# Attention b: where the rows that hold a softmax's maxima are cleared, written and copied

## The chip, the cores and the metric

The kernel runs on one core of a Trainium2 chip. The metric is the time of one execution on the device in microseconds. The core has five engines that work side by side: PE multiplies matrices and transposes, DVE, ACT and POOL do vector work, and SP only issues transfers (DMAs). Each engine runs its instructions in order; an instruction that waits holds up all that is queued behind it on that engine.

## The reference

Four layers on x of 2 x 512 x 512 (batch, sequence, width), each added to its input behind a layer norm:

```python
x = L0_attn_a_hidden_states
x = x + _L0_attn_a_ref(_layernorm(x), ...)   # 32 heads of 128, 8 for keys and values, int4 weights
x = x + _L0_ffn_ref(_layernorm(x), ...)      # 8 experts of rank 64, the best 2 of each row
x = x + _L0_attn_b_ref(_layernorm(x), Wq, Wk, Wv, Wo)
x = x + _L0_ffn_ref(_layernorm(x), ...)      # the same experts
```

The change lies in attention b, which has heads of only 16 elements:

```python
q = (resid @ Wq).reshape(B, T, 32, 16)       # k and v: 8 heads, each shared by 4 of q
q, k = q * cos + rotate_half(q) * sin, k * cos + rotate_half(k) * sin
att = einsum('bhgqd,bhkd->bhgqk', q, k) / sqrt(16)
probs = softmax(where(causal, att, -inf))
out = einsum('bhgqk,bhkd->bhgqd', probs, v).reshape(B, T, 512) @ Wo
```

## The kernel before

**Stages.** Attention a runs from 0 to about 735 us, with the first experts of batch 0 mixed in near its end, and is not touched. Then come the first experts of batch 1 (`experts(1, "f1")`) with the projections of attention b for batch 0 (to about 809 us), the loop of attention b (to about 1056 us), and a tail: the output projection of the last heads (`output_b(1, (2, 3))`) and the second experts of batch 1. The experts of batch 0 for the second time, the projections of batch 1 and the rest of the output projection are *side work*: generators from which the loop takes some units in each step.

**What the loop does.** It goes over 32 pairs of heads `p` = (batch b, half of the key heads `kh`, group `g`, `pr`), three steps a pair. A pair's softmax needs each row's maximum before the exponentials, and both the maximum and the subtraction are brought into matmuls. A query is kept as a high part, rounded to PE's fast 32-bit form (`fp32r`), and the low rest; keys likewise. Four copies of 16 rows (query high, low, high, low against key high, high, low, low) make 64 rows, so that one matmul over them has all four products. Behind these lie two more rows (`HALF` = 64 to `HM` = 66): -1 in the keys' tile `ks` (L588), and in the queries' tile `qs` first zeros, later the row's maximum as a high and a low part. So a matmul with zeros there gives the scores, and one with the maxima there gives scores less the maximum. For each pair, in the order of its life:

- `queries_halved(p)` (L724 to 733), once per four pairs, at a step in which another pair's load is due: ACT rounds the queries to `hl` (L729), POOL takes the low rest (L730), and two transfers (`spread`, L711) write both to a buffer in DRAM, each row twice. The pool `dram` has two buffers for each such name.
- `queries_in(p)` (L735 to 740), four steps ahead of the pair's first step: one transfer loads 64 rows of 4 KB into `qs[p % 5]`; from the sixth pair on POOL clears rows 64 and 65 (L740), since an earlier pair has left its maxima there.
- `maxima()` (L742 to 774), three steps: PE's `sc_b` (L758) are scores of the queries against the keys up to the diagonal, for query tiles 0 and 1 in the first step, 3 in the second and 2 in the third. DVE reduces each to its rows' maxima, `top` (L762). Behind the last, POOL writes the maxima's high part (L770) and low part (L771) to two columns of `mm`, first of one head, then of the other: columns 64 and 65 for the first head, 0 and 1 for the second.
- `maxima_in(p)` (L776 to 784), at step 3p + 4 (`step - 4` in the loop), ahead of that step's other work on PE: four transpositions of `mm` into one bank, `tpm` (L781), and one ACT copy for each head from there to `qs` (L784).
- `probabilities()` (L789 to 825), from step 3p + 8 (`LEAD`): `st_b` (L805), keys against queries with the maxima's rows; ACT's exponential to `pT_b` (L811); POOL's causal mask on the diagonal tiles (L814).
- `weighted_b` (L824 to 855): `num_b` (L831), values and a column of ones against `pT_b`, for two pairs at a time; its results' denominators go by `dens_b` transfers to one tile. Then `divided` (L860 on: two reciprocals on DVE, and what they multiply) and `output_b` (L878 on).

**What sets the order.** Inside the loop PE's order is the one written in the program (`manual_schedule`, PE alone); the other engines' order is placed by a scheduler from the dependencies. In a step PE gets: `maxima_in`, then the step's `st_b`, its `sc_b`, the `num_b` that are due, and then side work. How much of that is set by `pace`, added to `left` in every step; each unit of side work takes its own worth away, mostly `MM` = 0.9. The pace is 1.05 at the start, 0.38 from step 44, 1.05 from step 66 and 1.5 from step 90; the loop has 96 + 8 steps. After the last step some side work (`parts(side, 6)`) stands ahead of `output_b(1, (2, 3))`, which needs the last quotients.

**Rings.** `qs` has five tiles, `mm` two. `sc_b`, `st_b` and `tpm` share five banks of PSUM (`ps_x`); side work in the loop has two others (`ps_f`), and outside the loop it uses the five. `we` (L254) holds the gate's weight of each expert, spread over its 64 ranks, for one tile of 128 rows; POOL writes it, PE transposes it to `wT_f`. Its pool has two tiles for the four of a batch. `pT_b` tiles 512 wide have a ring of five.

The lines around the step that moves:

```python
            p, at = divmod(step - 4, STEPS)
            if at == 0 and 0 <= p < len(pairs):
                maxima_in(p)
            if LEAD <= step:
                next(ps)        # probabilities: st_b
            if step < total:
                next(ms)        # maxima: sc_b
```

Of the kernel before, what the change touches and what calls it, by code (L numbers as in the profile page):

```python
# [11 lines left out]
F32 = mybir.dt.float32  # L12
# [7 lines left out]
P = 128  # L20
# [20 lines left out]
def kernel(  # L41
# [533 lines left out]
    HALF, HM = P // 2, P // 2 + 2  # L575
# [11 lines left out]
    for pad in ks:  # L587
        nc.gpsimd.memset(pad[HALF:HM], -1.0)  # L588
# [10 lines left out]
    dram = ctx.enter_context(tc.tile_pool(name="dram", bufs=2, space=bass.MemoryType.DRAM))  # L599
    ptp = ctx.enter_context(tc.tile_pool(name="pT2", bufs=6))  # L600
# [3 lines left out]
    homes.update(xT=(xtp, "xnT"), xn=(temps, "t"), hT=(hp, "hT"), we=(wep, "we"))  # L604
# [102 lines left out]
    def spread(hl, nm, order):  # L707

        to = dram.tile([4, P, S], F32, tag=f"spread{nm[0]}", name=f"spread_{nm}")
        for twice in range(2):  # L710
            nc.sync.dma_start(  # L711
                to[order[twice]].rearrange("n r s -> r n s"), hl.bitcast(F32)
            )
        return to.rearrange("n (d h) s -> (n d) h s", h=B_NKV)

    kparts, qparts = {}, {}

    def keys_in(b, kh):

        if kh == 0:  # L720
            kparts[b] = spread(khls[b], f"k_{b}", (slice(0, 4, 2), slice(1, 4, 2)))
        nc.sync.dma_start(ks[kh][:HALF], kparts[b][:, ts(kh, 4), :])

    def queries_halved(p):  # L724

        b, kh, g, _ = pairs[p]
        hl = hlp.tile([P, 2, S], F32R, tag="hl", name=f"hl_{p}")
        src = qTs[b][:, kh * 2 + g // 2, :]
        nc.scalar.copy(hl[:, 0, :], src)  # L729
        nc.gpsimd.tensor_tensor(hl[:, 1, :], src, hl[:, 0, :].bitcast(F32), ALU.subtract)  # L730
        to = spread(hl, f"q_{p}", (slice(0, 2), slice(2, 4)))
        for n in range(4):
            qparts[p + n] = to

    def queries_in(p):  # L735
        _, _, g, pr = pairs[p]
        q = qs[p % NQ]
        nc.sync.dma_start(q[:HALF], qparts.pop(p)[:, ts((g % 2) * 2 + pr, 2), :])
        if p >= NQ:
            nc.gpsimd.memset(q[HALF:HM], 0.0)  # L740

    def maxima():  # L742

        for p, (b, kh, g, pr) in enumerate(pairs):
            q, k = qs[p % NQ].bitcast(F32R), ks[kh].bitcast(F32R)
            top = small.tile([P, NT, 2], F32, tag="top", name=f"top_{p}")
            for tiles in ((0, 1), (3,), (2,)):
# [18 lines left out]
                if tiles == (2,):  # L766
                    mm = mms[p] = mmp[p % len(mmp)]
                    for h in range(2):
                        at = (1 - h) * HALF
                        nc.gpsimd.tensor_copy(mm[:, :, at], top[:, :, h])  # L770
                        nc.gpsimd.tensor_tensor(  # L771
                            mm[:, :, at + 1], top[:, :, h], mm[:, :, at].bitcast(F32), ALU.subtract
                        )
                yield

    def maxima_in(p):  # L776

        mm = mms.pop(p).bitcast(F32)
        tp = ps_x.tile([P, S], F32, tag="x", name=f"tpm_{p}")
        for t in range(NT):  # L780
            nc.tensor.transpose(tp[:HM, ts(t, P)], mm[:, t, :], ident)  # L781
        for h in range(2):
            at = (1 - h) * HALF
            nc.scalar.copy(qs[p % NQ][HALF:HM, h, :].bitcast(F32R), tp[at : at + 2, :])  # L784
# [136 lines left out]
    banks[:] = BESIDE  # L921
    side = chain(later, projections(1))
    pace, left = 1.05, 0.0
    for step in range(total + LEAD):
        with tc.manual_schedule(engines={mybir.EngineType.PE}):
# [8 lines left out]
            if step == half + LEAD + 10:  # L934
                side = chain(side, output_b(0, (2, 3)), experts(0, "f2", True))
                pace, left = 1.05, 0.0
            if step == total - 6:
                side = chain(output_b(1, (0, 1)), side)
                pace, left = 1.5, 0.0
# [6 lines left out]
            p, at = divmod(step - 4, STEPS)  # L946
# [22 lines left out]
    parts(side, 6)  # L969
    run(output_b(1, (2, 3)))  # L970
    run(side, experts(1, "f2", True))
# [90 lines left out]
```

## Time and profile before

| | |
|---|---|
| median of three runs | 1117.19 us (1116.21 to 1117.54) |
| the profiled execution, its time | 1118.06 us |
| its span, first to last instruction | 1116.3 us |
| mean granted clock of PE | 0.992 of full speed |
| PE busy | 1060.7 us, 95% of the span, 4940 instructions |
| PE's weight loads (beside its matmuls) | 708.8 us, 63% |
| DVE busy | 880.8 us, 79% |
| ACT busy | 617.4 us, 55% |
| POOL busy | 587.4 us, 53% |
| chain that ended last, by engine | PE 80%, DVE 10%, ACT 3%, POOL 3%, issue 2%, DMA 1% |

By stage, busy us of each engine:

| stretch, us | what | length | PE | DVE | ACT | POOL | clock |
|---|---|---|---|---|---|---|---|
| 0 to 735 | attention a | 735 | 704.7 | 646.9 | 439.1 | 430.3 | 1.00 |
| 736 to 808 | first experts of batch 1, projections of batch 0 | 72 | 68.3 | 36.6 | 15.3 | 27.9 | 0.98 |
| 808 to 832 | start of the loop | 24 | 21.1 | 20.6 | 11.7 | 8.4 | 0.79 |
| 832 to 1056 | the rest of the loop | 224 | 212.5 | 150.1 | 142.9 | 118.5 | 1.00 |
| 1056 to 1117 | tail | 61 | 53.1 | 25.6 | 8.4 | 2.3 | 0.96 |

An engine's busy time is the time in which it executes something; the rest of a stretch it waits, for another engine, a bank, a transfer or its own order. The clock is the share of its full speed that PE was granted. In the groups, `qs<-tpm 2x512` is an operation that reads `tpm` and writes `qs`, 2 partitions by 512 elements; a name after `<-` in a wait is the engine and the tile that ended it.

### The profile page before, as it was taken

The numbers are of one execution on the slowest core, as the hardware profiler recorded it, in microseconds if no ns is written. First come the engines' busy times: TensorE is split into PE (matmuls) and PEld (weight loads), VectorE is DVE, ScalarE is ACT, GpSimd is POOL, SyncE is SP. The second block draws the span as 40 slices with busy tenths as digits, with TensorE's granted clock in tenths as the row PEclk, the third lists the DMA queues.
The fourth block names the chain that finished last, engine by engine and source line by source line (L and its number), as shares of the span: only waits on it lengthen the run. The fifth ranks groups of instructions, "written<-read, shape, count | busy, mean of one in ns | idle before, by whom it ended". The sixth has DMA issues, their size and how long they took to land.

```text
span 1116.3 us, 16200 instructions
## 1 busy us (share of the span) xinstructions
PE 1060.7 (95%) x4940; PEld 708.8 (63%) x4940; DVE 880.8 (79%) x2195; ACT 617.4 (55%) x1421; POOL 587.4 (53%) x920
## 2 busy tenths in 40 slices
PE   5799999999999999999999999999989989999988
PEld 3467677777777777777777777546457555555543
DVE  6889899999999999999999889574376677877252
ACT  3556566577566566566565665513157566585410
POOL 2557566666656656756756666261245566454200
PEclk9999999999999999999999999999989999999999
DMA  7301011022010010010021000042342235111000
GB/s 288 114 1 38 1 38 38 1 76 68 9 39 24 15 38 14 26 38 8 32 76 38 1 1 1 1 156 63 91 156 77 61 106 152 44 44 26 10 33 38
DMA packets 21030, 58.11 MB, mean 52 GB/s; under 512 B 3152, under 2 KB 4112, under 8 KB 18128
## 3 DMA queue, kind: packets, MB, share of 16 engines
q1 hardware_dynamic: 20944, 57.08, 15.6%
q8 instruction: 40, 0.66, 0.2%
q14 instruction: 46, 0.38, 0.1%
HBM read 43.30 MB, written 12.58 MB: 50 GB/s over the span
## 4 chain that ended last, share of the span: by engine, by line
PE 80%; DVE 10%; ACT 3%; POOL 3%; issue 2%; DMA 1%; SPq 0%; ACTq 0%; DVEq 0%; POOLq 0%
PE av L429 11%; PE sc L396 11%; PE tp L424 5%; PE ps_o L439 5%; PE ps_o L438 5%; PE ps_q L358 5%; PE ph_f L207 5%; PE ps_q L359 5%; PE num_b L831 3%; PE st_b L805 3%; PE py_f L266 3%; PE sc_b L758 3%; PE pq_b L678 2%; PE po L885 2%; DVE r_q L365 2%
## 5 line engine op out<-in xcount | busy, mean ns | idle before, releaser
L404 ACT ACTIVATE p<-sc,nmx 128x128 f32<-128x128 f32 (+3 forms) x256 | 135.7, 530 | 95.1 <-DVE nmx L399 92.1
L376 POOL TENSOR_TENSOR r_q<-r_q,tab 128x512 f32<-128x512 f32 x64 | 82.5, 1289 | 190.2 <-DVE rs_q L375 190.2
L396 PE MATMUL sc<-kT,qT 128*128 128x128 f32 (+3 forms) x512 | 180.0, 433 | 1.2 <-POOL qT L377 0.9
L365 DVE SCALAR_TENSOR_TENSOR r_q<-ps_q,s_q,r_q 128x512 f32<-128x512 f32 x192 | 143.4, 747 | 36.1 <-PE ps_q L359 22.4
L413 POOL TENSOR_SCALAR p<-p,rden 128x128 f32<-128x128 f32 (+3 forms) x256 | 140.3, 562 | 58.5 <-DVE rden L411 24.5
L425 ACT COPY pT<-tp 128x128 f32<-128x128 f32 (+3 forms) x256 | 109.4, 428 | 104.1 <-PE tp L424 103.5
L762 DVE CUSTOM_DVE_ANT_0 sc_b<-sc_b,tri 128x128 f32<-128x128 f32 (+3 forms) x256 | 119.6, 516 | 47.3 <-PE sc_b L758 42.5
L429 PE MATMUL av<-pT,v 128*128 128x512 f32 (+3 forms) x512 | 148.5, 433 | 0.0
L429 PEld LDWEIGHTS av<-pT,v 128*128 128x128 f32 x512 | 97.0, 190 | 80.2 <-issue 53.9
L448 DVE SCALAR_TENSOR_TENSOR acc<-ps_o,s_o,acc 128x512 f32<-128x512 f32 x186 | 137.3, 738 | 5.5 <-PE ps_o L439 5.4
L399 DVE CUSTOM_DVE_ANT_0 sc<-sc,tri 128x128 f32<-128x128 f32 (+3 forms) x256 | 125.1, 489 | 8.1 <-PE sc L396 7.3
L358 PE MATMUL ps_q<-xh,w_q 128*128 128x512 f32 x256 | 122.7, 479 | 7.6 <-DVE r_q L365 7.6
L424 PE MATMUL tp<-ident,p 128*128 128x128 f32 x640 | 112.9, 272 | 2.6 <-POOL p L413 2.6
L396 PEld LDWEIGHTS sc<-kT,qT 128*128 128x128 f32 x512 | 95.6, 189 | 25.3 <-ACT p L404 2.0
L438 PE MATMUL ps_o<-ah,w_o 128*128 128x512 f32 x256 | 107.9, 422 | 1.7 <-DVE acc L448 1.0
L811 ACT ACTIVATE pT_b<-st_b 128x384 f32<-128x384 f32 (+1 forms) x192 | 90.1, 528 | 34.4 <-PE st_b L805 33.5
L439 PE MATMUL ps_o<-al,w_o 128*128 128x512 f32 x256 | 104.8, 410 | 3.5 <-DVE al L152 3.5
L424 PEld LDWEIGHTS tp<-ident,p 128*128 128x128 f32 x640 | 83.0, 141 | 30.7 <-issue 6.4
L359 PE MATMUL ps_q<-xl,w_q 128*128 128x512 f32 x256 | 101.2, 395 | 0.0
L814 POOL TENSOR_SCALAR_AFFINE_SELECT pT_b<-pT_b 128x128 f32<-128x128 f32 (+1 forms) x192 | 62.2, 333 | 64.7 <-ACT pT_b L811 62.2
L377 POOL TENSOR_TENSOR qT<-r_q,rs_q 128x512 f32<-128x512 f32 x64 | 85.5, 1335 | 1.0
L446 POOL TENSOR_TENSOR acc<-acc,part 128x512 f32<-128x512 f32 x62 | 79.9, 1288 | 10.2 <-ACT part L445 10.1
(182 smaller groups left out, 2065.4 us busy)
## 6 DMA issues: line engine op xcount, KB each, us to landing
codes_q<-in_q_codes_dram SPq DMA_DIRECT2D x8, 1024.0 KB
codes_o<-in_o_codes_dram SPq DMA_DIRECT2D x8, 1024.0 KB
spread_q<-hl SPq DMA_DIRECT2D x16, 512.0 KB
qs<-spread_q SPq DMA_DIRECT2D x32, 256.0 KB
x_a<-in_x_dram SPq DMA_DIRECT2D x8, 256.0 KB
codes_k<-in_k_codes_dram SPq DMA_DIRECT2D x2, 1024.0 KB
codes_v<-in_v_codes_dram SPq DMA_DIRECT2D x2, 1024.0 KB
x_r<-in_x_dram SPq DMA_DIRECT2D x8, 256.0 KB
```

The costliest lines, as they stand in the source:

```text
L358: nc.tensor.matmul(ps, w[:, c, ts(h, A_HD)], xh[b][:, c, :], start=True, stop=False)
L359: nc.tensor.matmul(ps, w[:, c, ts(h, A_HD)], xl[b][:, c, :], start=False, stop=True)
L365: nc.vector.scalar_tensor_tensor(r, ps, s, r, ALU.mult, ALU.add)
L396: nc.tensor.matmul(sc[:, :n], qT[:, ts(i, P)], kT[:, :n], start=True, stop=True)
L399: nc.vector.tensor_tensor_reduce(sc[:, :n], sc[:, :n], tri[:, S - n :], -(A_HD**-0.5), 3e38, ALU.add, ALU.min, nmx,)
L404: nc.scalar.activation(pr, sc[:, :n], AF.Exp, bias=nmx, scale=-1.0, accum_out=den[:, i % 2 : i % 2 + 1],)
L413: nc.gpsimd.tensor_scalar(prs[j], prs[j], rden[:, j % 2 : j % 2 + 1], 1.0, ALU.mult, ALU.mult)
L424: nc.tensor.transpose(tp[:, j, :], prs[i][:, ts(j, P)], ident)
L429: nc.tensor.matmul(av[:, j * P :], v[:, j, :], pT[:, j, j * P :], start=(j == 0), stop=(j == NT - 1))
L438: nc.tensor.matmul(ps, w[:, h, ts(n, P)], ah, start=True, stop=False)
L439: nc.tensor.matmul(ps, w[:, h, ts(n, P)], al, start=False, stop=True)
L448: nc.vector.scalar_tensor_tensor(to, ps, s, to, ALU.mult, ALU.add)
```

## The change

In words, in the order of the diff:

- The maxima get four rows for two (`HM` = 68): two for each head of the pair. In `ks`, rows 64 and 65 are -1 in the first head's columns and 0 in the second's, rows 66 and 67 the other way round. So both heads' query halves may hold all four rows. Eight memsets write these in place of two.
- The pool `dram` has one buffer for each name, and the names are fixed tiles: one for the keys, two for the queries by turns. The queries' have 4 rows more for each of the 8 key heads; two transfers at the start fill these with zeros.
- `queries_in` loads 68 rows in place of 64, the last four of them zeros, and the memset behind it is gone.
- The maxima of both heads are written in two POOL operations on every other column in place of four, and copied to `qs` in one ACT copy of 4 x 1024 in place of two of 2 x 512.
- `maxima_in` comes one step later, at step 3p + 5.
- The experts' weights `we` use the ring of `pT_b`'s 512-wide tiles (five) before and after the loop; in the loop they keep their own ring of two.
- The paces are 0.95 for 1.05 from step 66 and 1.35 for 1.5 from step 90, and 8 parts of side work for 6 stand ahead of the last output projection.

```diff
@@ -572,7 +572,8 @@
 
 
 
-    HALF, HM = P // 2, P // 2 + 2
+    HALF, HM = P // 2, P // 2 + 4
     NQ = 5
     qs = [w2.tile([P, 2, S], F32, tag=f"qs{n}", name=f"qs_{n}") for n in range(NQ)]
     ks = [w2.tile([P, 4, S], F32, tag=f"ks{n}", name=f"ks_{n}") for n in range(2)]
@@ -585,7 +586,9 @@
     for pad in (*ks, *qs, *vpads, *(mm.bitcast(F32) for mm in mmp)):
         nc.gpsimd.memset(pad, 0.0)
     for pad in ks:
-        nc.gpsimd.memset(pad[HALF:HM], -1.0)
+        for h in range(2):
+            nc.gpsimd.memset(pad[HALF:HM, h : 4 : 2, :], -float(h))
+            nc.gpsimd.memset(pad[HALF : HALF + 2, h : 4 : 2, :], h - 1.0)
     for pad in vpads:
         for t in range(NT):
             for kh in range(2):
@@ -596,12 +599,12 @@
     bp = ctx.enter_context(tc.tile_pool(name="b", bufs=1))
     hp = ctx.enter_context(tc.tile_pool(name="hT", bufs=1))
     hlp = ctx.enter_context(tc.tile_pool(name="hl", bufs=1))
-    dram = ctx.enter_context(tc.tile_pool(name="dram", bufs=2, space=bass.MemoryType.DRAM))
-    ptp = ctx.enter_context(tc.tile_pool(name="pT2", bufs=6))
+    dram = ctx.enter_context(tc.tile_pool(name="dram", bufs=1, space=bass.MemoryType.DRAM))
+    ptp = ctx.enter_context(tc.tile_pool(name="pT2", bufs=5))
     ps_x = ctx.enter_context(tc.tile_pool(name="ps_x", bufs=5, space=PSUM))
     ps_n = ctx.enter_context(tc.tile_pool(name="ps_n", bufs=1, space=PSUM))
     ps_f = ctx.enter_context(tc.tile_pool(name="ps_f", bufs=2, space=PSUM))
-    homes.update(xT=(xtp, "xnT"), xn=(temps, "t"), hT=(hp, "hT"), we=(wep, "we"))
+    homes.update(xT=(xtp, "xnT"), xn=(temps, "t"), hT=(hp, "hT"), we=(ptp, f"pT{S}"))
 
     ALONE, BESIDE = [(ps_x, "x")], [(ps_f, "f")]
     banks[:] = ALONE
@@ -704,22 +707,28 @@
 
 
 
-    def spread(hl, nm, order):
-        to = dram.tile([4, P, S], F32, tag=f"spread{nm[0]}", name=f"spread_{nm}")
-        for twice in range(2):
-            nc.sync.dma_start(
-                to[order[twice]].rearrange("n r s -> r n s"), hl.bitcast(F32)
-            )
-        return to.rearrange("n (d h) s -> (n d) h s", h=B_NKV)
-    kparts, qparts = {}, {}
+    kspread = dram.tile([HALF * B_NKV, S], F32, tag="kspread", name="kspread")
+    qspread = [
+        dram.tile([HM * B_NKV, S], F32, tag=f"qspread{n}", name=f"qspread_{n}") for n in range(2)
+    ]
+    for to in qspread:
+        nc.sync.dma_start(to[HALF * B_NKV :], qs[0][: (HM - HALF) * B_NKV, 0, :])
+    def spread(to, hl, parts):
+        to = to[: HALF * B_NKV].rearrange("(n r) s -> n r s", r=P)
+        for part in parts:
+            nc.sync.dma_start(to[part].rearrange("n r s -> r n s"), hl.bitcast(F32))
+    def spread_heads(to):
+        return to.rearrange("(r h) s -> r h s", h=B_NKV)
 
     def keys_in(b, kh):
 
         if kh == 0:
-            kparts[b] = spread(khls[b], f"k_{b}", (slice(0, 4, 2), slice(1, 4, 2)))
-        nc.sync.dma_start(ks[kh][:HALF], kparts[b][:, ts(kh, 4), :])
+            spread(kspread, khls[b], (slice(0, 4, 2), slice(1, 4, 2)))
+        nc.sync.dma_start(ks[kh][:HALF], spread_heads(kspread)[:, ts(kh, 4), :])
 
     def queries_halved(p):
 
@@ -728,16 +737,12 @@
         src = qTs[b][:, kh * 2 + g // 2, :]
         nc.scalar.copy(hl[:, 0, :], src)
         nc.gpsimd.tensor_tensor(hl[:, 1, :], src, hl[:, 0, :].bitcast(F32), ALU.subtract)
-        to = spread(hl, f"q_{p}", (slice(0, 2), slice(2, 4)))
-        for n in range(4):
-            qparts[p + n] = to
+        spread(qspread[p // 4 % 2], hl, (slice(0, 2), slice(2, 4)))
 
     def queries_in(p):
         _, _, g, pr = pairs[p]
-        q = qs[p % NQ]
-        nc.sync.dma_start(q[:HALF], qparts.pop(p)[:, ts((g % 2) * 2 + pr, 2), :])
-        if p >= NQ:
-            nc.gpsimd.memset(q[HALF:HM], 0.0)
+        at = (g % 2) * 2 + pr
+        nc.sync.dma_start(qs[p % NQ][:HM], spread_heads(qspread[p // 4 % 2])[:, ts(at, 2), :])
 
     def maxima():
 
@@ -765,12 +770,9 @@
                     )
                 if tiles == (2,):
                     mm = mms[p] = mmp[p % len(mmp)]
-                    for h in range(2):
-                        at = (1 - h) * HALF
-                        nc.gpsimd.tensor_copy(mm[:, :, at], top[:, :, h])
-                        nc.gpsimd.tensor_tensor(
-                            mm[:, :, at + 1], top[:, :, h], mm[:, :, at].bitcast(F32), ALU.subtract
-                        )
+                    high, low = mm[:, :, HALF:HM:2], mm[:, :, HALF + 1 : HM : 2]
+                    nc.gpsimd.tensor_copy(high, top)
+                    nc.gpsimd.tensor_tensor(low, top, high.bitcast(F32), ALU.subtract)
                 yield
 
     def maxima_in(p):
@@ -779,9 +781,8 @@
         tp = ps_x.tile([P, S], F32, tag="x", name=f"tpm_{p}")
         for t in range(NT):
             nc.tensor.transpose(tp[:HM, ts(t, P)], mm[:, t, :], ident)
-        for h in range(2):
-            at = (1 - h) * HALF
-            nc.scalar.copy(qs[p % NQ][HALF:HM, h, :].bitcast(F32R), tp[at : at + 2, :])
+        both = tp[HALF:HM].unsqueeze(1).to_broadcast([HM - HALF, 2, S])
+        nc.scalar.copy(qs[p % NQ][HALF:HM].bitcast(F32R), both)
 
 
     due = []
@@ -918,7 +919,7 @@
     ms, ps = maxima(), probabilities()
     total = len(pairs) * STEPS
     half = total // 2
-    banks[:] = BESIDE
+    banks[:], homes["we"] = BESIDE, (wep, "we")
     side = chain(later, projections(1))
     pace, left = 1.05, 0.0
     for step in range(total + LEAD):
@@ -933,17 +934,17 @@
                 keys_in(1, 1)
             if step == half + LEAD + 10:
                 side = chain(side, output_b(0, (2, 3)), experts(0, "f2", True))
-                pace, left = 1.05, 0.0
+                pace, left = 0.95, 0.0
             if step == total - 6:
                 side = chain(output_b(1, (0, 1)), side)
-                pace, left = 1.5, 0.0
+                pace, left = 1.35, 0.0
             quotients[:] = [q for q in quotients if next(q, None) is not None]
             p, at = divmod(step + 4, STEPS)
             if at == 0 and p % 4 == 3 and p + 1 < len(pairs):
                 queries_halved(p + 1)
             if at == 0 and 2 <= p < len(pairs):
                 queries_in(p)
-            p, at = divmod(step - 4, STEPS)
+            p, at = divmod(step - 5, STEPS)
             if at == 0 and 0 <= p < len(pairs):
                 maxima_in(p)
             if LEAD <= step:
@@ -966,8 +967,9 @@
         weighted_b(*due.pop(0)[1])
 
     run(*quotients)
-    parts(side, 6)
+    parts(side, 8)
     run(output_b(1, (2, 3)))
+    homes["we"] = ptp, f"pT{S}"
     run(side, experts(1, "f2", True))
```

## The prediction

> **What bounds the kernel now.** I read the page first: PE is busy 95% of the span, so the only things worth asking about a change outside PE's own work are where PE stands idle and who ends each wait. The whole change lies after 736 us, so next I cut that stretch into stages. Columns: stretch, its length, then busy us of PE, PEld, DVE, ACT and POOL, then the granted clock, DMA share and GB/s.
>
> ```profile
> 808.00:832.00 24.00, 21.09 (x77) 13.87 (x76) 20.60 (x78) 11.73 (x20) 8.35 (x25) 0.79 0.46 142
> 832.00:892.00 60.00, 59.09 (x376) 38.63 (x375) 39.37 (x155) 38.52 (x86) 34.70 (x98) 1.00 0.29 85
> 892.00:962.00 70.00, 62.19 (x402) 37.14 (x401) 53.15 (x191) 45.70 (x94) 42.94 (x119) 1.00 0.36 111
> 962.00:1056.00 94.00, 91.21 (x555) 52.36 (x555) 57.54 (x206) 58.69 (x116) 40.82 (x126) 1.00 0.11 28
> 1056.00:1080.00 24.00, 20.84 (x59) 9.52 (x61) 15.98 (x28) 3.92 (x6) 0.00 (x0) 0.93 0.11 39
> ```
>
> PE's idle time is 2.9, 0.9, 7.8, 2.8 and 3.2 us: 11.5 us in the loop of attention b (832 to 1056), most of it from 892 to 962, where little side work is mixed in. No other engine is full there (DVE 53 of 70), so these are waits of a chain and not of a full engine. The waits view of PE from 820 to 1062 (us in total, times, longest) names them:
>
> ```profile
> PE tpm L781 <- POOL mm L771: 7.0, 8, 1.9
> PE sc_b L758 <- ACT qs L784: 3.1, 4, 0.9
> PE sc_b L758 <- ACT pT_b L811: 1.3, 2, 0.8
> PE st_b L805 <- ACT qs L784: 0.6, 2, 0.3
> ```
>
> The largest is the transposition of a pair's maxima waiting for POOL to write them; the next is the copy behind that transposition, which gives the PSUM bank back late. The groups say what POOL and ACT do for it (busy us, mean ns, then idle before):
>
> ```profile
> L784 ACT CAST qs<-tpm 2x512 fp32r<-2x512 f32 x62 | 35.7, 575 | 33.1 <-PE tpm L781 32.7
> L740 POOL MEMSET qs<- 2x1024 f32 x27 | 25.5, 946 | 25.4 <-PE st_b L805 25.3
> L771 POOL TENSOR_TENSOR mm<-top,mm 128x4 fp32r<-128x4 f32 x61 | 13.4, 220 | 3.9
> L770 POOL CAST mm<-top 128x4 fp32r<-128x4 f32 x60 | 11.9, 199 | 9.4 <-DVE top L762 7.8 <-DVE oh_f L238 0.6
> ```
>
> One of these waits, in order of time:
>
> ```profile
> 906.47 0.19 POOL L770 CAST mm<-top 128x4 fp32r<-128x4 f32 x1
> 906.74 0.21 POOL L771 TENSOR_TENSOR mm<-top,mm 128x4 fp32r<-128x4 f32 x1
> 906.89 0.29 POOL L814 TENSOR_SCALAR_AFFINE_SELECT pT_b<-pT_b 128x128 f32<-128x128 f32 x1
> 907.14 0.19 POOL L770 CAST mm<-top 128x4 fp32r<-128x4 f32 x1
> 907.42 0.21 POOL L771 TENSOR_TENSOR mm<-top,mm 128x4 fp32r<-128x4 f32 x1
> 907.68 0.63 PE L781 MATMUL tpm<-ident,mm 128*66 128x128 f32 x4 [1.12 <-POOL mm L771]
> 908.89 0.95 POOL L740 MEMSET qs<- 2x1024 f32 x1 [0.78 <-PE st_b L805]
> ```
>
> Four small operations with a mask between them take POOL from 906.47 to 907.63, and PE waits 1.12 us for the last.
>
> **Part by part.** *Transposition one step later (`step - 5`).* PE issues it behind that step's `st_b` and `sc_b` instead of ahead of them: the four `st_b` and two `sc_b` behind the wait above start at 908.06 and 908.60 and last to 909.2, so some 1.2 us of ready work, and the side work of the step, now come first. Two POOL operations for four shorten the chain by about 0.4 + 0.3 us (199 + 220 ns, and the gaps). Of the 7.0 us, 1.94 belong to the start at 820 (below), which leaves 5.06. One wait of 1.08 us, at 946, I keep as not gained: there DVE runs its two reciprocals (1735 ns each) without a break ahead of the maxima, and PE would stop at the next bank that DVE holds. That leaves 4.0. The bank waits on the copy (3.1 + 0.6 = 3.7 us) are half of this kind (the 0.95, 0.79 and 0.79 us ones lie behind reciprocals), so I take half, 1.85. Ends: 2.0 (half of the 4.0, nothing of the banks) and 8.8 (all). Value: **-5.85**. The copy is still due before `st_b` of its pair, three steps on; at 6.67 us for three steps (66.7 us for the ten pairs from 892.3 to 959.0) that is no new wait.
>
> *One copy for two.* No row has 4x1024. The 128x512 copy takes 588 ns and the 128x128 one 269, so 0.83 ns for each further element: 588 + 512 x 0.83 = 1013 ns against 2 x 575. ACT gains 0.14 us a pair and is busy 58.69 of 94: nothing but the earlier bank, counted above.
>
> *27 memsets gone.* 25.5 us of POOL, and 25.3 us in which it stood in order behind PE's `st_b` with the masks of `pT_b` queued behind it. PE hardly waits for those masks (0.2 us at `num_b`), so by itself: 0. It is part of why the maxima come late, and that is counted.
>
> *Memsets of `ks`.* Two of 2.0 us become eight of about 0.95 (the 2x1024 row): +3.6 us from 747 on. POOL's next work with a deadline starts at 765.06 after 12.2 us of idling: 0. The two transfers of zeros are issued on SP ahead of the keys' spread at 775.1, where SP has nothing to do: 0.
>
> *Weights' ring.* The last two of four `we` copies no longer wait for a transposition in the first and last stage (the loop keeps its ring of two). PE's waits on `wT_f` there are 0.29 at 799.7 and 0.37 at 1097.7. The second is **-0.37**; the first only brings the start forward: POOL subtracts `hl` at 799.80, when ACT's cast ends, instead of behind the copies at 800.15.
>
> *Paces.* 24 steps at 0.95 for 1.05 and 14 at 1.35 for 1.5 put off (2.4 + 2.1) / 0.9 = 5 units of about 0.86 us, 4.3 us of PE. PE is 97% busy there, so the loop ends that much earlier. Behind the last `num_b`, the order of instructions after the change has 8 transpositions and 8 matmuls of 0.86, 8.1 us, in place of 9 matmuls, 8.0 us (1055.26 to 1063.26), to cover the last quotients, and the other 3.4 us later. Value 0; if the loop did not shorten, +4.3.
>
> *The queries' transfer, 68 rows for 64.* Its waits and its place on SP stay, but for the spread of the fourth group (`hl_12`), which now queues behind the load of pair 7 and has until pair 12. What a row costs shows in a transfer that runs alone, issued at 828.32 (same columns as above):
>
> ```profile
> 829.50:829.75 0.25, 0.25 (x2) 0.17 (x1) 0.25 (x2) 0.17 (x2) 0.25 (x1) 0.50 0.97 147
> 829.75:830.00 0.25, 0.25 (x2) 0.25 (x2) 0.25 (x1) 0.25 (x1) 0.25 (x2) 0.50 0.96 197
> 830.25:830.50 0.25, 0.25 (x3) 0.15 (x2) 0.15 (x1) 0.25 (x1) 0.23 (x1) 0.50 0.62 229
> 830.75:831.00 0.25, 0.25 (x3) 0.25 (x2) 0.25 (x3) 0.25 (x1) 0.24 (x1) 0.50 0.20 49
> ```
>
> It starts 1.2 us after its issue and is over in 1.5. Shares (0.97, 0.96, 0.62, 0.62, 0.63, 0.20) x 0.25 us x 16 engines = 16.0 us of engine time for 64 rows, 0.25 each; in the steady part 0.62 x 16 engines at 229 GB/s, 56 rows of 4 KB a us, 0.18 each. How many engines 68 rows use no row shows. Bounds: all 16 (1.5 x 68/64 = 1.6 us) or four, the most that the four rows of a `dens_b` transfer can occupy: 17 rows each, 3.1 us at 0.18, 4.25 at 0.25. I take four at 0.18, since 68 is 4 x 17 as 64 is 16 x 4.
>
> The Trainium skill speaks against the change here: "DMA: Bandwidth & Descriptors", section "Why a DMA increments its semaphore by 16 and not by 1", says that a copy is spread over the largest number of engines up to 16 that divides its outer size, which is 16 for 64 rows and 4 for 68. By it the sum is the one made here; with all 16 engines it would be 1.2 us lower; no run so far shows which holds.
>
> In the loop a load is issued 7.2 us (pair 16, 911.4 to 918.6) to 14 us ahead of its first `sc_b`, and 1.2 + 3.1 = 4.3, or 5.5, fits: 0. The start has no such room. Before, PE reaches the first `sc_b` at 809.37 without a wait, with the load issued at 805.64. After: issue 805.3, landing 809.6: +0.25. Three loads go out together, 51 rows an engine, 9.4 us, to 815.9; the second spread queues behind them and takes its 2.9 us: 818.8 instead of about 814.1. ACT's cast of `hl_8` waits for it (0.62), POOL's subtraction next (1.27), and the maxima of pair 1 are queued behind that on POOL: 820.7 + 0.4 = 821.1, against 820.16 for the transposition before. Value **+0.9**; ends -0.3 (all 16 engines: only the earlier start) and +4.3 (0.25 a row: 819.3 + 2.9 + 1.9 + 0.4 = 824.5).
>
> *Clock.* After the thin stretch at 818 to 822 the granted clock is 0.50 until 832; two 128x512 `sc_b` take 0.85 there against 0.6 outside, so some 2.0 of the 6.4 us from 825.6 to 832 hang on it. The thin stretch stays about as thin: 0; ends -2.0 and +1.0.
>
> **Sum.** -5.85 - 0.37 + 0.9 = -5.3. The profiled execution took 1118.1 for its span of 1116.3 and lies 0.9 above the median of 1117.2; from the median the forecast is **1111.9**. Own range 1107.5 to 1115.
>
> **Rivals.** *The waits go but the next takes their place (1116.2).* For it: 53 of 70 us of DVE, five banks shared by `sc_b`, `st_b` and `tpm`, and a `sc_b` wait on `top` of 0.7 us that is already there. Against: DVE has gaps next to most of the waits (0.98 us at 903, 0.55 at 906). A quarter of the 5.85 stays: -1.5 - 0.4 + 0.9 = -1.0. *Slower: the 68-row loads hold four engines (1120.5).* Place: the start, through `hl_8` on ACT and POOL. Price +4.3 with 0.25 us a row, the clock +1.0 for another thin stretch, while the loop gives its lower 2.0: +3.3. It decides from some 0.25 us a row, and in the loop too once a landing passes 7.2 us, 0.35 a row. For it: no wait hides the first load. Against: the steady part shows 0.18. *The change does not reach PE*: if POOL's order, not the step, made the waits, they would stay; the order of instructions shows the transposition moved in all 32 pairs, so I give it no chance of its own.
>
> **How the numbers follow.** Forecast 0.65, next wait 0.17, slower 0.18. I call 0.2% (2.2 us) what a measurement here can tell from no change: faster 0.66, same 0.16, slower 0.18. The range goes from 1106.5 (8.8 in the loop, part of the clock) to 1120, just short of the slower rival.
>
> **What would show it.** Right: PE's wait for `mm` under 2 us, idle time from 892 to 962 under 4 us in a shorter stage, no `L740`. The start: first `sc_b` with a wait of about 0.5 us, `hl_8` cast near 819, 68-row transfers of about 3 us at a DMA share near 0.25. Wrong: `sc_b` waiting for DVE `top` or for `qs` by DMA in the loop by more than 3 us, or a first `st_b` past 824.

## The result, and the profile after

The changed kernel takes 1120.94 us (median of nine runs, 1118.04 to 1122.60) against 1116.30 us before (nine runs beside it): a ratio of 1.0042 with a 95% interval of 1.0032 to 1.0052. It is slower by 4.6 us, where 5.3 us of gain were forecast, and lies 0.9 us above the stated range, which ends at 1120. The profiled execution took 1120.94 us, with a span of 1119.2 and a mean granted clock of 0.988 (0.992 before).

The stages of the changed kernel (stretch, length, busy us of PE, PEld, DVE, ACT and POOL, granted clock, DMA share, GB/s):

```profile
808.00:832.00 24.00, 19.18 (x65) 11.66 (x64) 18.17 (x72) 8.94 (x14) 5.67 (x14) 0.80 0.39 141
892.00:962.00 70.00, 62.04 (x387) 36.16 (x385) 52.30 (x186) 43.74 (x83) 30.69 (x87) 0.98 0.30 100
1056.00:1080.00 24.00, 20.71 (x53) 9.93 (x52) 15.31 (x27) 2.20 (x6) 0.00 (x0) 0.86 0.08 28
```

PE's idle time at the start of the loop is 4.8 us for 2.9, and from 892 to 962 it is 8.0 us for 7.8: the stage that was to gain gained nothing, though POOL is busy 30.7 us there for 42.9. The clock column shows something more: 0.98 in the middle of the loop and 0.86 in the tail, for 1.00 and 0.93. PE's waits from 806 to 1062 (us in total, times, longest):

```profile
PE st_b L806 <- ACT qs L785: 3.8, 5, 2.0
PE sc_b L763 <- ACT pT_b L812: 3.8, 8, 1.0
PE sc_b L763 <- issue: 2.4, 1, 2.4
PE sc_b L763 <- ACT qs L785: 1.8, 5, 0.5
PE st_b L806 <- ACT pT_b L812: 1.5, 6, 0.4
PE tpm L783 <- POOL mm L775: 0.5, 1, 0.5
```

The wait for the maxima fell from 7.0 to 0.5 us, as forecast. But the waits of `st_b` and `sc_b` for ACT (rows 1, 2, 4 and 5) are 10.9 us for the 5.4 of before (the 3.1, 1.3 and 0.6 among the prediction's rows, and the row below), and a new one of 2.4 us stands at the first `sc_b`.

```profile
PE st_b L805 <- ACT pT_b L811: 0.4, 1, 0.4
```

The groups of the changed kernel, and behind them the last row's counterpart before:

```profile
L785 ACT CAST qs<-tpm 4x1024 fp32r<-4x1024 f32 x32 | 32.1, 1004 | 38.1 <-PE tpm L783 36.2 <-DMA oN_b<-o_b 1.5
L774 POOL CAST mm<-top 128x8 fp32r<-128x8 f32 x32 | 6.7, 208 | 20.2 <-DVE top L767 15.4 <-DVE rstd_f L168 3.3 <-DVE mv_b L164 1.4
L738 ACT CAST hl<-qT 128x512 fp32r<-128x512 f32 x8 | 5.0, 619 | 27.0 <-DMA qspread<-hl 24.3 <-issue 2.7
```

```profile
L729 ACT CAST hl<-qT 128x512 fp32r<-128x512 f32 x8 | 5.0, 620 | 13.8 <-DMA spread_q<-hl 13.7
```

The one copy takes 1004 ns (1013 were estimated) and a POOL operation on both heads hardly more than one on one head (208 ns for 199). The rows of `hl` are the ones to see: ACT stood 24.3 us in front of the queries' rounding, waiting for the spread of the group before (13.7 before).

**The start.** From the timeline of the changed kernel, PE's first `sc_b`, and ACT's rounding of the third group of queries with the copies behind it (start, us, then the idle time before it and what ended it); last, the same two operations before:

```profile
810.90 0.70 PE L763 MATMUL sc_b<-ks,qs 128*128 128x128 f32 x4 [2.44 <-issue]
```

```profile
819.07 0.62 ACT L738 CAST hl<-qT 128x512 fp32r<-128x512 f32 x1 [13.44 <-DMA qspread<-hl]
820.61 1.01 ACT L785 CAST qs<-tpm 4x1024 fp32r<-4x1024 f32 x1 [0.93 <-PE tpm L783]
```

```profile
809.37 0.70 PE L758 MATMUL sc_b<-ks,qs 128*128 128x128 f32 x4
814.13 0.62 ACT L729 CAST hl<-qT 128x512 fp32r<-128x512 f32 x1 [7.83 <-DMA spread_q<-hl]
```

The load for that `sc_b` was issued at 804.96 and PE began 5.9 us later. The profile names nothing that ended this wait (`issue`); in the kernel below that loads 64 rows and 4 rows, a wait of 0.47 us at the same place ends with the queries' load. Windows over this stretch:

```profile
809.00:810.00 1.00, 0.00 (x0) 0.00 (x0) 0.00 (x0) 0.00 (x0) 0.00 (x0) 1.00 1.03 360
813.00:815.00 2.00, 2.00 (x4) 0.99 (x3) 0.60 (x1) 0.00 (x0) 0.00 (x0) 0.50 0.25 96
817.00:819.00 2.00, 2.00 (x10) 1.24 (x9) 2.00 (x12) 0.00 (x0) 0.39 (x2) 1.00 0.27 105
```

At 809 all 16 DMA engines are busy while every compute engine stands still: the second spread, issued at 807.00, runs while the first load is not yet over. The small packets that close a transfer (they are counted under "Engines or bytes") show when it ends. From 809.40 to 810.45 four are moved, all between 809.9 and 810.2:

```profile
DMA packets 181, 0.40 MB, mean 380 GB/s; under 512 B 4, under 2 KB 4, under 8 KB 181
```

Taken as those of the first load, they come 4.9 to 5.2 us behind its issue; a load that runs alone, issued at 830.13, has its four between 834.2 and 834.6, 4.1 to 4.5 us behind. So the load ends some 0.8 us later than alone, and another 0.7 us pass before PE starts. Then, until 822, the share is 0.25 at about 100 GB/s, four engines of 16, while the other loads and the rest of the spread go through them. The rounding of the third group waits for this until 819.07 (814.13 before).

**The loop.** The same happens at the second batch, and there PE pays for it. In order of time, from the ACT and the PE rows of the stretch 941 to 950:

```profile
944.91 0.62 ACT L738 CAST hl<-qT 128x512 fp32r<-128x512 f32 x1 [2.12 <-DMA qspread<-hl]
945.55 1.00 ACT L785 CAST qs<-tpm 4x1024 fp32r<-4x1024 f32 x1
946.61 0.44 PE L806 MATMUL st_b<-qs,ks 128*128 128x384 f32 x1 [1.97 <-ACT qs L785]
```

Before, ACT comes to the rounding of this group without a wait:

```profile
934.90 0.62 ACT L729 CAST hl<-qT 128x512 fp32r<-128x512 f32 x1
```

At 934.6 to 936.4 SP had issued a spread, the keys' load, a load of queries and the second half of the spread. ACT's rounding needs that half to have been read, since `hl` has one buffer; it stands at the head of ACT's queue until 944.91, and the copy of another pair's maxima stands behind it. PE waits 1.97 us for a copy whose input it had itself finished at 943.84. Not every such stop is paid: ACT also stands 3.15 us ahead of the rounding at 911.90, which costs PE nothing, and 2.65 us ahead of the one at 925.34, which costs PE 0.82.

### The profile page after: what moved, and what is told of

It is laid out like the page before. It is cut to its first block, busy times and chain, and to the rows that moved or that the text cites. A ratio compares the mean times of both kernels' runs of the same rounds, so it can differ in the third digit from the quotient of the medians.

```text
span 1119.2 us, 16020 instructions
## 1 busy us (share of the span) xinstructions
PE 1063.2 (95%) x4940; PEld 711.4 (64%) x4940; DVE 878.6 (79%) x2195; ACT 610.5 (55%) x1389; POOL 556.5 (50%) x835
## 4 chain that ended last, share of the span: by engine, by line
PE 78%; DVE 11%; ACT 4%; issue 2%; DMA 2%; POOL 1%; SPq 0%; ACTq 0%; DVEq 0%; POOLq 0%
PE av L429 11%; PE sc L396 10%; PE tp L424 5%; PE ps_o L439 5%; PE py_f L266 5%; PE ps_o L438 5%; PE ph_f L207 5%; PE ps_q L358 5%; PE ps_q L359 4%; PE sc_b L763 3%; PE st_b L806 3%; PE num_b L832 3%; PE pq_b L681 3%; PE po L886 2%; DVE r_q L365 2%
```

## The experiments

All ratios are against the kernel before, run beside each on the same chip. The change and fifteen other kernels:

| kernel | ratio | 95% interval |
|---|---|---|
| the change, 68 rows | 1.0042 | 1.0032 to 1.0052 |
| the change, 80 rows | 0.9968 | 0.9956 to 0.9980 |
| before, with the 68-row transfer alone | 1.0069 | 1.0056 to 1.0081 |
| before, with an 80-row transfer alone | 1.0000 | 0.9988 to 1.0012 |
| 68 rows, `step - 4` | 1.0043 | 1.0030 to 1.0055 |
| 68 rows, paces of before | 1.0047 | 1.0034 to 1.0059 |
| 68 rows, rounding on POOL | 0.9993 | 0.9984 to 1.0003 |
| 80 rows, `step - 4` | 0.9962 | 0.9950 to 0.9974 |
| 80 rows, paces of before | 0.9965 | 0.9952 to 0.9978 |
| 80 rows, both of these | 0.9961 | 0.9946 to 0.9976 |
| 80 rows, two copies | 0.9980 | 0.9969 to 0.9992 |
| 80 rows, four POOL operations | 0.9973 | 0.9962 to 0.9984 |
| 80 rows, weights' ring of before | 0.9984 | 0.9974 to 0.9993 |
| 80 rows, `step - 4`, rounding on POOL | 0.9967 | 0.9955 to 0.9979 |
| 72 rows | 0.9960 | 0.9945 to 0.9975 |
| 64 rows and 4 rows, two transfers | 0.9942 | 0.9926 to 0.9958 |

**80 rows for 68.** The order of instructions is the changed kernel's on every engine but SP, where only sizes differ.

```diff
+    LOAD = 80
...
-        dram.tile([HM * B_NKV, S], F32, ...)
+        dram.tile([LOAD * B_NKV, S], F32, ...)
...
-        nc.sync.dma_start(to[HALF * B_NKV :], qs[0][: (HM - HALF) * B_NKV, 0, :])
+        nc.sync.dma_start(to[HALF * B_NKV :], qs[0][: (LOAD - HALF) * B_NKV, 0, :])
...
-        nc.sync.dma_start(qs[p % NQ][:HM], ...)
+        nc.sync.dma_start(qs[p % NQ][:LOAD], ...)
```

> The changed kernel with 80 rows in the queries' transfer for 68 (80 = 16 x 5; the twelve further rows are zeros); the order on PE, DVE, ACT and POOL is the same. Theory 'four engines' (a transfer of 68 rows runs on four of 16 engines, so that what is issued behind it is late): DMA share near 1 in these transfers, first sc_b within 0.5 us of 809, the cast of hl_8 on ACT near 814 to 815, no stop of ACT of over 1 us at a cast of hl after 900; 0.994 to 0.999 of the time before, about 1110 to 1115 us. Rival 'next wait' (what the transposition gained is taken by waits for banks and for ACT's longer copy): within 0.1% of the changed kernel, 1.003 to 1.005. Rival 'side work' (the paces and the tail cost it): the same 1.003 to 1.005.

1113.02 us, 0.9968. With 18% more bytes in each load the kernel is 0.74% faster, some 8 us, and faster than the kernel before. The first `sc_b` starts at 808.45, 4.0 us behind the issue of its load; the rounding of the third group is at 813.01; and at the second batch ACT comes to the rounding without a wait:

```profile
808.45 0.70 PE L764 MATMUL sc_b<-ks,qs 128*128 128x128 f32 x4 [0.51 <-issue]
813.01 0.62 ACT L739 CAST hl<-qT 128x512 fp32r<-128x512 f32 x1 [7.88 <-DMA qspread<-hl]
938.44 0.61 ACT L739 CAST hl<-qT 128x512 fp32r<-128x512 f32 x1
```

One sign did not come as expected: ACT still stands 3.25 us ahead of the rounding at 908.80, the stop that costs PE nothing in the changed kernel either. Against the changed kernel the first `sc_b` of a pair comes earlier by 2.5 us at pair 0, 3.0 at pair 4 (830.87 for 833.86), 3.1 at pair 15 and 7.2 at pair 22 (955.43 for 962.59): less the 0.5 us by which the load is issued later (804.96 for 804.46), some 2.5 us are lost at the start, and 4 at the second batch. Of the 4, 1.0 come between pairs 15 and 17, 1.7 between 19 and 20, behind the stop at 946, and 1.2 from there to pair 21, where PE was granted half its speed (last section).

**Before, with the 68-row transfer alone.** No memset, as in the change; everything else as before. The buffers in DRAM are fixed tiles, two for the keys and two for the queries, so as many as before, with rows of zeros that two transfers fill at the start.

```diff
...
-        nc.sync.dma_start(q[:HALF], qparts.pop(p)[...])
-        if p >= NQ:
-            nc.gpsimd.memset(q[HALF:HM], 0.0)
+        nc.sync.dma_start(q[:LOAD], qparts.pop(p)[...])     # LOAD = 68
```

> The kernel before with nothing but the queries' transfer of the change: 68 rows, the last four of them zeros from a buffer in DRAM that two transfers fill at the start, and no memset behind it. Theory 'four engines': first sc_b at 811 or later for 809.4, the cast of hl_8 near 819 for 814, ACT stopped behind later casts of hl; slower than before by 3 to 6 us, 1.003 to 1.005. Rivals 'next wait' and 'side work': the transfer is hidden, 0.999 to 1.001.

1123.83 us, 1.0069: 7.7 us slower, more than expected. The first `sc_b` waits 1.9 us and starts 5.7 us behind the issue of its load. It is at 809.01 and the rounding of the third group at 817.03, both earlier than expected; but in this profile all was earlier already ahead of the loop (the first `pkv_b` of the projections at 759.22 for 761.58 before), and with these 2.4 us added both are where they were expected. So the transfer costs about 8 us in either kernel.

**The step moved back, and the paces, with 68 rows.** Each by itself:

```diff
-            p, at = divmod(step - 5, STEPS)
+            p, at = divmod(step - 4, STEPS)
```

```diff
-                pace, left = 0.95, 0.0
+                pace, left = 1.05, 0.0
...
-                pace, left = 1.35, 0.0
+                pace, left = 1.5, 0.0
...
-    parts(side, 8)
+    parts(side, 6)
```

> The changed kernel with the transposition back at the step it had (step - 4). Theory 'four engines': the move itself gains, so this is slower than the changed kernel by 1 to 4 us, 1.005 to 1.008 of the time before, with PE's wait for mm (POOL) back at 3 us or more. Rival 'next wait': the move gains nothing or costs, 1.001 to 1.004.

> The changed kernel with the paces (1.05, 1.5) and the six parts ahead of the last output projection of before. Theory 'four engines': as the changed kernel within 1 us, 1.003 to 1.005. Rival 'side work': the work that was put off is what costs, 1.000 to 1.002.

1.0043 and 1.0047: neither undoing moves the time; for the step the theory had expected 1.005 to 1.008. With `step - 4` PE's wait for `mm` is back at 7.1 us, ten times, and costs nothing more in all.

**The rounding on POOL.**

```diff
-        nc.scalar.copy(hl[:, 0, :], src)
+        (nc.gpsimd.tensor_copy if p else nc.scalar.copy)(hl[:, 0, :], src)
```

> The changed kernel, 68 rows as in it, with the rounding of the queries (hl) on POOL for ACT from the second group on; PE's order is the same. Theory 'ACT's queue' (the late transfers reach PE because ACT's cast of hl waits for the last spread with the copy of the maxima queued behind it): no wait of st_b for qs of over 1 us after 900, PE's idle time from 892 to 962 falls by 2 us or more, 1.000 to 1.003 of the time before; the start gains at most 1 us, since the first load is as late as it was. Rival 'any queue' (POOL then stops with masks and maxima behind it, and PE waits for those instead): 1.004 or more.

0.9993, a little better than expected and some 5.5 us better than the change with the transfers as they were. POOL now stands where ACT stood, and PE hardly feels it; POOL's row and PE's:

```profile
942.51 0.61 POOL L738 CAST hl<-qT 128x512 fp32r<-128x512 f32 x1 [3.21 <-DMA qspread<-hl]
```

```profile
941.25 0.44 PE L806 MATMUL st_b<-qs,ks 128*128 128x384 f32 x1 [0.29 <-ACT qs L785]
```

The spread is late as before, but the copy is no longer queued behind it: PE waits 0.29 us for 1.97, and the longest wait that follows up to 946 is one of 0.73 us. PE is busy 63.67 of the 70 us from 892 to 962 for 62.04, 1.6 us more where 2 were expected. The first `sc_b` begins at 809.14 for 810.90, still with a wait of 2.2 us; 1.5 of these 1.8 us stand already ahead of the loop (the first `pkv_b` at 759.68 for 761.18), so the start itself gained 0.3 us, within the 1 us expected. What is left to the kernel with 80 rows, 0.25% or 2.8 us, is about what the start lost there.

**The parts, with 80 rows.** Each is undone by itself: the move and the paces as above, then the one copy, the two POOL operations and the ring; and the transfer is tried without the rest (as above, with `LOAD` = 80).

```diff
-        both = tp[HALF:HM].unsqueeze(1).to_broadcast([HM - HALF, 2, S])
-        nc.scalar.copy(qs[p % NQ][HALF:HM].bitcast(F32R), both)
+        for h in range(2):
+            nc.scalar.copy(qs[p % NQ][HALF:HM, h, :].bitcast(F32R), tp[HALF:HM])
```

```diff
-                    nc.gpsimd.tensor_copy(high, top)
-                    nc.gpsimd.tensor_tensor(low, top, high.bitcast(F32), ALU.subtract)
+                    for h in range(2):
+                        at = HALF + 2 * h
+                        nc.gpsimd.tensor_copy(mm[:, :, at], top[:, :, h])
+                        nc.gpsimd.tensor_tensor(mm[:, :, at + 1], top[:, :, h], ...)
```

```diff
-    homes.update(..., we=(ptp, f"pT{S}"))
+    homes.update(..., we=(wep, "we"))
-    banks[:], homes["we"] = BESIDE, (wep, "we")
+    banks[:] = BESIDE
-    homes["we"] = ptp, f"pT{S}"
```

> 80 rows in the queries' transfer, and the transposition back at step - 4. Theory 'the move gains once the transfers are out of the way': slower than with the move (0.9968) by 2 to 5 us, 0.9985 to 1.001 of the time before, PE's wait for mm back at 5 us or more. Rival 'the next wait has eaten it': 0.996 to 0.998.

> 80 rows, and the paces (1.05, 1.5) and six parts of before. Theory 'the paces are worth nothing': within 1 us of the kernel with 80 rows, 0.996 to 0.998. Rival 'side work': the 4.3 us of work that were put off behind the loop cost there, 0.993 to 0.995.

> 80 rows, and the one ACT copy of 4x1024 split in two of 4x512, a head each. Theory 'the one copy costs nothing': within 1 us of the kernel with 80 rows, 0.996 to 0.998 (0.15 us more of ACT a pair, off the path). Rival 'longer copy' (the 1.0 us copy in one piece holds ACT's exponentials, and these give the banks back late: 5.7 us of PE's waits end with pT_b): 0.9945 to 0.996, since the first head's st_b may start half a copy earlier.

> The kernel before with the queries' transfer of 80 rows that clears the maxima's rows, and no memset: all other work and all orders are those of the run with 68 rows. Theory 'sum of parts' (the remaining parts of the change gave 0.27% with 68 rows, from 1.0069 to 1.0042, and give the same here): 0.9985 to 1.0005 of the time before. Rival 'memset' (the 27 memsets of POOL are what the change gains by): 0.996 to 0.998.

> 80 rows, and the maxima written by four POOL operations of 128x4 for two of 128x8. Theory 'POOL's chain counts': slower than the kernel with 80 rows (0.9968) by 1 to 3 us, 0.9975 to 0.9995 of the time before, PE's wait for mm still under 2 us but more waits for qs. Rival 'memset' or 'ring': 0.996 to 0.998.

> 80 rows, and the experts' weights in their own ring of two throughout, as before. Theory 'ring' (the start of the loop comes earlier, and the last stage is shorter): slower than the kernel with 80 rows by 0.7 to 1.5 us, 0.9974 to 0.9982 of the time before, PE's waits for we_f back at 0.3 to 0.4 us twice. Rival: within 0.05% of 0.9968.

The move is worth nothing (0.9962 without it), nor are the paces (0.9965), nor the memsets: the kernel before with the 80-row transfer and no memset stands at 1.0000 (the two were not tried apart). The other three effects point one way and are small: without the one copy 0.9980, without the two operations 0.9973, without the ring 0.9984. The first two lie within the uncertainty of two such comparisons, and the ring's 0.16% is at its edge; the POOL operations were expected to cost 1 us at least and show 0.6; together the three make up 0.12 + 0.05 + 0.16 = 0.33%, which is what the change gains with 80 rows (0.32%); a kernel with these three and without the move and the paces (0.9961, below) has all of the gain. The two copies were to be faster by a rival and were not. Where the move's gain went, the waits show. First the 80-row kernel without the move, then with it, both from 806 to 1062:

```profile
PE tpm L784 <- POOL mm L776: 6.5, 9, 1.9
PE sc_b L764 <- ACT pT_b L813: 2.6, 5, 0.8
PE sc_b L764 <- ACT qs L786: 1.8, 3, 0.8
PE st_b L807 <- ACT pT_b L813: 0.5, 2, 0.4
PE st_b L807 <- ACT qs L786: 0.3, 2, 0.2
```

```profile
PE sc_b L764 <- ACT pT_b L813: 4.2, 10, 1.0
PE sc_b L764 <- ACT qs L786: 1.6, 4, 0.5
PE st_b L807 <- ACT pT_b L813: 1.5, 6, 0.4
PE st_b L807 <- ACT qs L786: 1.4, 4, 0.6
PE tpm L784 <- POOL mm L776: 0.6, 1, 0.6
```

The move takes 5.9 us from the wait for `mm` and puts 3.5 us on the waits for ACT's exponentials and copies (5.2 to 8.7): the copy now comes a step later, right ahead of its own `st_b` and in the row of exponentials that give the banks back. The 2.4 us that this leaves did not show in the time. The granted clock from 962 to 1056 is 0.96 in the profile with the move and 1.00 in the one without, and over all runs of these two kernels its mean is 0.9905 and 0.9934, which could hide them; but 72 rows with the move have 0.9921 and no better time than 80 rows without it, so that stays open.

**Both undone, and the rounding on POOL as well.**

> 80 rows, the transposition at step - 4 and the paces and six parts of before together: of the change there remain the two POOL operations, the one copy, the ring of the weights and the cleared rows. Theory 'move and paces are worth nothing': 0.9955 to 0.9972, as the kernels with 80 rows. Rival 'each hides the other': 0.998 or more.

> 80 rows, the transposition at step - 4, and the rounding of the queries on POOL from the second group on. Theory 'ACT's queue': a gain over the same without the last edit (0.9962) of 0.5 to 2 us, 0.9945 to 0.9958. Rival 'nothing left': with 16 engines the spread is no longer late, 0.9955 to 0.997.

0.9961: the move and the paces do not hide each other. 0.9967: with 16 engines nothing is left to gain on ACT's queue.

**Engines or bytes.** 72 rows (`LOAD` = 72), and the 68 rows in two transfers:

```diff
-        nc.sync.dma_start(qs[p % NQ][:HM], spread_heads(...)[:, ts(at, 2), :])
+        rows = spread_heads(...)[:, ts(at, 2), :]
+        for part in (slice(0, HALF), slice(HALF, HM)):
+            nc.sync.dma_start(qs[p % NQ][part], rows[part])
```

> The changed kernel with 72 rows in the transfer for 68. Theory 'engines by division': 72 = 12 x 6, so a load that runs alone has a DMA share near 0.75, takes under 2 us, and the time is that of 80 rows, 0.996 to 0.9985. Rival 'bytes' or 'any count that 16 does not divide': share near 0.25 or the 68 rows' time, 1.003 or more.

> The changed kernel with its 68 rows in two transfers, 64 rows and then 4; PE's order is the same. Theory 'engines' (the number of engines that a transfer takes decides, not what it carries): the 64 rows run on 16 engines, 0.996 to 0.9985 of the time before, no stop of ACT at a cast of hl with a wait of st_b for qs of over 1 us. Rival 'bytes or rows': as the changed kernel, 1.003 or more. 32 issues more on SP, about 0.25 us each, may cost up to 1 us at the start.

72 rows: 0.9960. 64 and 4: 0.9942, 6.4 us faster than before, more than expected and the lowest of all, though its interval overlaps those of 72 rows and of most kernels with 80. The DMA view of a load that runs alone counts engines directly: besides the rows of 4 KB there are small packets that close the transfer. First 68 rows (the change), then 72, then 80:

```profile
DMA packets 72, 0.28 MB, mean 70 GB/s; under 512 B 4, under 2 KB 4, under 8 KB 72
```

```profile
DMA packets 84, 0.29 MB, mean 113 GB/s; under 512 B 12, under 2 KB 12, under 8 KB 84
```

```profile
DMA packets 96, 0.33 MB, mean 149 GB/s; under 512 B 16, under 2 KB 16, under 8 KB 96
```

Less the small ones they are 68, 72 and 80 rows, and the small ones are 4, 12 and 16: one for each engine, if the DMA share is read with it: about 0.25 in the first and up to 0.75 in the second.

## Why the prediction was wrong, by its steps

- **The queries' transfer, +0.9: the step that failed.** That 68 rows take four engines was right, and so was their price: alone, the load issued at 830.13 runs from 831.2 to 834.4, 3.2 us for 3.1. Two things were missed. At the start the first load was to land before the second spread began, and PE to begin as it landed; it ended some 0.8 us later than alone, with two more loads and the spread issued behind it (which of them takes most was not separated), and PE began 0.7 us after that: 5.9 us from issue to `sc_b` for the 4.3 of the sum (4.0 with 80 rows). Some 2.5 us were lost by pair 4. And "in the loop 0" asked only whether a load lands before its own `sc_b`. It does: no wait of PE in the loop ends with a load. What was not followed is what is queued behind the load: the spread, then the one buffer of `hl`, ACT's rounding, the copy of the maxima, `st_b`. That chain had been followed at the start, where it gave 818.8 for the rounding (819.07 measured), and was left out at the second batch, where it costs about 4 us. In all the transfer costs 0.69% alone and 0.74% in the change, about 8 us for the 0.9. With the rest of the change worth 0.32% (80 rows), that is +8.3 - 3.6 = +4.7 us where the sum had -5.3.
- **The transposition a step later: -5.85, measured 0.** This step failed too. The wait it names went (7.0 to 0.5 us). The rival "the next takes their place" is what happened to most of it (3.5 of 5.9 us with 80 rows), not at DVE's banks, as the rival had it, but at ACT; where the rest went was not shown. The earlier PSUM bank, counted in the same term, did not come either.
- **Two POOL operations and one copy: 0 for the copy.** Size right (1004 ns), and small gains of 0.05% and 0.12% from the runs, neither clear of the uncertainty.
- **Memsets: 0 by itself.** Right: 1.0000, together with the 80-row transfer.
- **Weights' ring: -0.37.** Sign right; undone it costs 0.16%, about 1.8 us, with intervals that overlap by 0.06%. More than the two waits of 0.3 and 0.4 us explain.
- **Paces: 0.** Right, with 68 rows and with 80.
- **Clock: 0, ends -2.0 and +1.0.** The upper end may have been low. Over all runs of one chip the mean clock is 0.9927 for the kernel before, 0.9886 for the 68-row kernels with one part undone and 0.9905 for the one with 80 rows. By these, PE lost at most 0.0041 x 1116 = 4.6 us and 2.5 us of full speed against before (an estimate, as if PE were never idle); what the clock did cost was not separated from the waits.
- **The slower rival** had the right mechanism, sign and place at the start. Its condition, 0.25 us a row, was not met (272 KB at about 100 GB/s are 2.8 us, 0.16 a row) and did not decide: what queues up behind the loads did. That its 1120.5 lies 0.4 us from the result is luck: it had +4.3 at the start, where 2.5 were lost, +1.0 by the clock and a gain of 2.0 in the loop, where 4 more were lost.
- **The signs of being wrong** did not show: `sc_b` waits 0.6 us for `top` and never for a load in the loop, and the first `st_b` is at 823.9. They named waits for the load itself and not for what stands behind it. Of the signs of being right, the waits for `mm`, the rounding of `hl_8` near 819 and the 68-row transfers came; the idle time from 892 to 962 (8.0 us for under 4) and the first `sc_b`'s wait (2.4 us for 0.5) did not.

## What to carry to other kernels

Before a transfer is reshaped, count the engines that it will run on and follow what is queued behind it on those engines, not only who reads what it brings: here four rows more in a load released the spread behind it at 819.07 for 813.01, and sending the four rows by themselves had the lowest time of all that was tried. A wait at the head of an in-order queue can be paid by the instruction behind it (two of the three stops in the loop were, here), so look for a one-buffer tile whose writer shares an engine with critical copies. A wait that is moved off one engine's path is gained only when the next instruction's own releaser is early too.

## What the runs showed of the hardware

The Trainium skill's page "DMA: Bandwidth & Descriptors", section "Why a DMA increments its semaphore by 16 and not by 1", which names the largest number of engines up to 16 that divides the rows, fits the counts 4, 12 and 16 for 68, 72 and 80 rows. Not expected: a transfer that is issued later does not wait for the whole of an earlier one. The second spread has all 16 engines busy at 809, and the first load, on four of them, is closed only by 810.2, some 0.8 us later than a load alone; so something issued behind it seems to have run on its four engines, too.

The clock was not expected either. These stretches of the changed kernel are the stop at 946 and what lies just behind it (columns as above; the granted clock is the third number from the end):

```profile
943.00:947.00 4.00, 2.03 (x10) 1.19 (x8) 2.62 (x6) 2.04 (x3) 1.52 (x2) 1.00 0.31 92
948.60:952.10 3.50, 3.50 (x9) 1.78 (x8) 3.50 (x13) 0.92 (x2) 1.20 (x5) 0.51 0.00 0
```

PE is busy for 2.03 of 4 us, its longest gap being the 1.97 us, and then granted half its speed for 3.5 us. The Trainium skill's page "TensorE: Matmul & The Clock Gate", section "Part 1: The HAM clock gate (the "warmup" mystery)", has the clock fall to half after an idle window of about 3.4 us. Here no gap is that long: PE was busy half of the time ahead of it. All four profiles with the 68-row loads and the rounding on ACT have such a stretch between 948 and 958, and of the other 13 only one (some have one elsewhere: the 80-row kernel between 962 and 1056). A stop of PE in the loop so seems to be paid a second time: with the rounding on POOL neither the stop nor the stretch is there. What sets these stretches off was not shown.
